# Weights split as rows and turned by transposing transfers, and another order of the head, in a gated feed-forward kernel with quantised activations

## The chip, the cores and the metric

One core of a Trainium2 chip runs the kernel; the other cores are idle. The metric is the device time of one execution in microseconds, the median of several runs. A profile of one execution shows what each engine did: TensorE (PE, with its weight loads as PEld), VectorE (DVE), ScalarE (ACT), GpSimd (POOL), and SyncE (SP), which here issues nearly all DMA transfers.

## What is computed

Cut to what matters, with B = 4 batches of S = 1024 tokens, D = 512, FF = 2048 and C = 128:

```
scale = cond @ norm_w.T + 1.0
ms = jnp.mean(x * x, axis=-1, keepdims=True)
h = x * (scale[:, None, :] * jax.lax.rsqrt(ms + EPS))
u = h @ up_w.T
val, gate = jnp.split(u, 2, axis=-1)
h = val * jax.nn.gelu(gate, approximate=False)
hq = h + stop_gradient(act_quant(h) - h)          # per token: round(x * 127 / max|x|), -128 to 127, back
wq = down_w + stop_gradient(weight_quant(down_w) - down_w)   # round(w / mean|w|), -1 to 1, back
y = hq @ wq.T
return y + x
```

All inputs and the output are float32. The first product must be nearly exact, because its result is rounded to integers.

## The kernel before

**Split products.** A float32 matrix is scaled by a power of two and split into two float16 parts, high and low ("w" counts the parts of the weights, "l" those of the tokens). A product is then the sum of high x high, high x low and low x high. The parts of the weights are wanted with D on the partitions, but `up_w` lies with FF as rows, so each block of weights has to be turned.

**Slots.** FF is cut into 16 blocks j of 128; a slot is one block of one batch of 1024 tokens, g = 16 b + j. Each slot has a gate block (t = 1) and a value block (t = 0).

**Batch 0** runs plain products (`plain`, `plain_half`): for each half of 512 tokens, 12 products for the gate into PSUM tag B or A, a Gelu on ScalarE, 12 products for the value into tag E (two banks), and one VectorE multiply (line 556) of value, gain and gate into `H`. While batch 0 runs, the weights of all 16 slots are prepared, two to four slots ahead (`first_batch`, slots 3 to 15):

- `w_load` brings 256 KB per t into `wn(j)`, one of three places; `w_range` finds each row's largest value on VectorE and its power of two (`w_factor`); `w_scale` scales the rows on GpSimd.
- `w_turn` turns the block on TensorE, 8 transposes of 128x128 float32 (line 296) into PSUM tag po. `w_high` (ScalarE) casts the high parts out of PSUM, `w_low` (VectorE) subtracts for the low parts; `w_evac` (ScalarE) copies the turned float32 to SBUF.
- `s_sums` makes four sums of the quarters of the block on GpSimd, `s_high` and `s_low` split them, and `s_spill` writes the slot's seven chunks (two float16 parts of 256 columns each) to `s_dram` in HBM in one transfer of 896 KB.
- Beside it the tokens of batch 1 are normalised, summed, split and turned by transposing transfers (`Tokens`: load, norm, scale, sums, high, low, turn), `down_w` is averaged and rounded (`d_load`, `d_sum`, `d_round`, `d_put`), and running maxima over pairs of slots are taken (`pair_max`).

**Batches 1 to 3** use seven products per slot in place of eight (a Strassen scheme, `slot` and `product`, 42 products of 512 columns in a slot of about 9.07 us), with the seven chunks read back from `s_dram`: `s_load_x` brings chunks 0 to 4 of slot g + 2, `s_load_y` chunks 5 and 6 of slot g + 1, both issued at the end of slot g. `SX` and `SY` say which chunk holds which operand. The second product (down) of the batch before runs inside slots 10 to 13.

**The head** prepares the first slot. Line 903 and what follows loads 8 tiles of tokens, `norm_w` and the weights of slots 0 to 2; warm products keep TensorE going; the sums of squares run on ScalarE, the reciprocal root (`rsqrt`) is a power on GpSimd, and the first 512 tokens are taken by quarters of the batch's half (two tiles of 128 at a time: `part_turn`, `part_high`, `part_low`, class `First`). Line 912 is a GpSimd power on a constant, ahead of the others.

**The order** of the work on every engine is the order of the program (`tc.manual_schedule()`): each engine and each DMA queue takes its instructions in that order and waits for what an instruction needs. SyncE's queue holds, in batch 0, the loads of weights, the spills, the turns of tokens and of `down_w`, and `cond_rows` in slot 3, three transfers of four-byte elements.

Of the kernel before, what the change touches and what calls it, by code (L numbers as in the profile page):

```python
# [14 lines left out]
ALU = mybir.AluOpType  # L15
# [22 lines left out]
SX = {0: 0, 1: 1, 4: 2, 5: 3, 6: 4}  # L38
# [12 lines left out]
def glu_quant_kernel(  # L51
# [81 lines left out]
    def s_tile(g):  # L133

        if g >= NJ:
            return SXY[:, (g + 1) % 2]
        return S_more if g % 3 == 2 else SXY[:, g % 3]
# [10 lines left out]
    def bank(tag, bufs, shape=None, name=None):  # L148
        return psum.tile(shape or [P, TOK], F32, name=name or tag, tag=tag, bufs=bufs)
# [102 lines left out]
    def wf(j):  # L252

        return H[:, 11 if j == 2 else 15 + j % 2].rearrange("p t (n f) -> p (t n) f", n=2)
# [3 lines left out]
    def w_load(j, ts=(1, 0)):  # L258
        for t in ts:
            SP.dma_start(out=wn(j)[:, t], in_=up_v[j][:, t])  # L260
# [21 lines left out]
    def w_scale(j, ts=(1, 0), eng=POOL):  # L282
        for t in ts:
            w, r = wn(j)[:, t], iv[j][:, t : t + 1]
            if eng is ACT:
                ACT.activation(w, w, AF.Copy, scale=r)
            else:
                eng.tensor_scalar(w, w, r, 1.0, ALU.mult, ALU.mult)  # L288
# [11 lines left out]
    def a_parts(j):  # L300

        s = s_tile(j)
        return s[:, 0:2], A21[:, j % 3], s[:, 5]
# [23 lines left out]
    def s_sums(j):  # L327
        a11, a12, a21, a22 = (wf(j)[:, n] for n in range(4))
        POOL.tensor_tensor(sf[:, 0], a21, a22, ALU.add)
        POOL.tensor_tensor(sf[:, 2], a11, a21, ALU.subtract)  # L330
        POOL.tensor_tensor(sf[:, 1], sf[:, 0], a11, ALU.subtract)
        POOL.tensor_tensor(sf[:, 3], a12, sf[:, 1], ALU.subtract)

    def s_parts(j):
        s = s_tile(j)
        return (s[:, 2:5], sf[:, 0:3]), (s[:, 6:7], sf[:, 3:4])
# [9 lines left out]
    def s_spill(j):  # L346
        SP.dma_start(out=s_dram[j], in_=s_tile(j).rearrange("p c w f -> p (c w f)"))

    CUT = 5 * 2 * HALF

    def s_load_x(g):
        s = s_tile(g)[:, 0:5].rearrange("p c w f -> p (c w f)")
        SP.dma_start(out=s, in_=s_dram[g % NJ, :, :CUT])

    def s_load_y(g):
        s = s_tile(g)[:, 5:7].rearrange("p c w f -> p (c w f)")
        SP.dma_start(out=s, in_=s_dram[g % NJ, :, CUT:])
# [181 lines left out]
    def gain(g, t):  # L539
        return sg[g // NJ][:, g % NJ, t : t + 1]  # L540

    def h_half(g, h):
        return h_slots(g)[:, 0, h]
# [14 lines left out]
    QT = TOK // 2  # L558

    class First:  # L560


        def __init__(self):
            self.ps = {1: bank("B", 1, name="pg_0_0"), 0: bank("A", 2, name="pv_0_0")}

        def part(self, t, q, w, l):
            gate, a21, a22 = a_parts(0)
            a = [gate[:, 0], gate[:, 1]] if t else [a21, a22]
            c = slice(q * QT, (q + 1) * QT)
            for k in range(NK):  # L570
                PE.matmul(
                    self.ps[t][:, c],
                    a[k // 2].rearrange("p w (k f) -> p w k f", k=2)[:, w, k % 2, :],
                    XP[:, l, k, c], start=w + l + k == 0, stop=l == 1 and k == NK - 1,
                )

        def gate(self):
            self.t1 = wpool.tile([P, TOK], F32, name="g_0_0", tag="t1")
            ACT.activation(self.t1, self.ps[1], AF.Gelu, scale=gain(0, 1))

        def value(self):
            DVE.scalar_tensor_tensor(
                h_half(0, 0), self.ps[0], gain(0, 0), self.t1, ALU.mult, ALU.mult
            )

# [249 lines left out]
    start_t = sm.tile([P, 1], F32, name="start_t", bufs=1)  # L835
    ACT.dma_start(out=cn, in_=cond[0:1])
    ACT.activation(start_t, one, AF.Gelu)
# [19 lines left out]

    def first_scale(n, eng):
        r = rs0[:, n : n + 1]
        if eng is ACT:  # L860
            ACT.activation(X0[:, n], X0[:, n], AF.Copy, scale=r)
        else:
            eng.tensor_scalar(X0[:, n], X0[:, n], r, 1.0, ALU.mult, ALU.mult)
# [5 lines left out]

    def part_turn(n, pts):  # L870
        for k in range(NK):
            c = k % 2 * QT + n % 2 * P
            PE.transpose(pts[k // 2][:, c : c + P], X0[:, n, k * P : (k + 1) * P], ident)

    def part_high(q, k, pts):
        c = slice(q * QT, (q + 1) * QT)
        v = pts[k // 2][:, k % 2 * QT : (k % 2 + 1) * QT]
        ACT.activation(XP[:, 0, k, c], v, AF.Copy, scale=scT[:, k, 0:1])

    def part_low(q, k, pts):  # L880
        c = slice(q * QT, (q + 1) * QT)
        v = pts[k // 2][:, k % 2 * QT : (k % 2 + 1) * QT]
        DVE.scalar_tensor_tensor(
            XP[:, 1, k, c], v, scT[:, k, 0:1], XP[:, 0, k, c], ALU.mult, ALU.subtract
        )
# [18 lines left out]
    SP.dma_start(out=nw, in_=norm_w.rearrange("(k p) c -> p k c", p=P))  # L904
    w_load(0, (1,))
    first_load(2, 2)
    w_load(0, (0,))
# [4 lines left out]
    POOL.tensor_tensor(rs0[:, 0:1], one, neghalf[:, 0:1], ALU.pow)  # L912
    keep_warm(3)
    pc = cond_first_row()
    keep_warm(7)
    first_sum(0)
    first_sum(1)
    cond_scale(0, pc)
    rsqrt(ssq0[:, 0:2], rs0[:, 0:2])
    mx = cond_largest(0, 1)  # L920
    pm = cond_over(mx, 0, 1, "A")
    am = w_largest(0, 1, 2)
    w_factor(0, am, 1, 2)
    first_scale(0, POOL)
    first_scale(1, ACT)
    dg = cond_range(pm, 0, 1)
    w_scale(0, (1,))
    ptx = [[po_bank("ptx_0_0"), po_bank("ptx_0_1")], [po_bank("ptx_1_0"), None]]
    part_turn(0, ptx[0])
    part_turn(1, ptx[0])  # L930
    pd = cond_spread(dg, 0, 1, "A")
    w_turn(0, [bank("E", 2, name=f"pw_0_{t}") for t in (1, 0)], (1,))
    ptx[1][1] = bank("A", 2, name="ptx_1_1")
    first_sum(2)
    first_sum(3)
    cond_undo(pd, 0, 1)
    rsqrt(ssq0[:, 2:4], rs0[:, 2:4])
    part_high(0, 0, ptx[0])
    w_high(0, (1,))
    for k in range(1, NK):  # L940
        part_high(0, k, ptx[0])
    first_scale(2, POOL)
    first_scale(3, POOL)
    w_low(0, (1,))
    w_range(0, 0, 1)
    w_scale(0, (0,))
    for k in range(NK):
        part_low(0, k, ptx[0])
    first = First()
    first.part(1, 0, 0, 0)  # L950
    first.part(1, 0, 1, 0)
    part_turn(2, ptx[1])
    part_turn(3, ptx[1])
    w_turn(0, ts=(0,))
    first.part(1, 0, 0, 1)
    w_high(0, (0,))
    for k in range(NK):
        part_high(1, k, ptx[1])
    w_gain(0)
    am = w_largest(1, 1, 2)  # L960
    w_low(0, (0,))
    for k in range(NK):
        part_low(1, k, ptx[1])
    w_factor(1, am, 1, 2)
    w_scale(1, (1,))
    w_range(1, 0, 1)
    w_gain(1)
    w_scale(1, (0,))
    cond_load_rest()
    for w, l in ((0, 0), (1, 0), (0, 1)):  # L970
        first.part(0, 0, w, l)
    for w, l in ((0, 0), (1, 0), (0, 1)):
        first.part(1, 1, w, l)
    first.gate()
    w_turn(1, ts=(1,))
    w_high(1, (1,))
    w_low(1, (1,))
    for w, l in ((0, 0), (1, 0), (0, 1)):
        first.part(0, 1, w, l)
    first.value()  # L980
    w_range(2)
    w_gain(2)
    w_scale(2)
    w_turn(1, ts=(0,))
    w_high(1, (0,))
    w_low(1, (0,))
# [12 lines left out]

    def first_batch(j, sc):  # L1000
# [5 lines left out]
        if j in TOKENS:  # L1006
            t = toks[j] = toks[j + 1] = Tokens(1, TOKENS[j])
            t.load()
        if j - 2 in TOKENS:
            toks[j - 2].turn()  # L1010
        t = toks.get(j)
        odd = t is not None and j not in TOKENS
        if j + 1 < NJ:
            s_sums(j + 1)
        if odd:
            t.sums()
        if j + 3 < NJ:
            w_range(j + 3)
            w_gain(j + 3)
            w_scale(j + 3)  # L1020
        if j == 5:
            part = d_total()
        plain_half(j, 0)
        if j == 3:
            pd = cond_spread(dg, 1, B, "po")
            cond_undo(pd, 1, B)
            cond_rows()
# [4 lines left out]
        if j + 1 < NJ:  # L1032
            s_high(j + 1)
            s_low(j + 1, POOL)
            s_spill(j + 1)
        if j + 2 < NJ:
            w_turn(j + 2)
            w_high(j + 2)
            w_evac(j + 2)
            w_low(j + 2)  # L1040
        plain_half(j, 1)
        if j == 5:
            d_mean(part)
        for i, h in pairs[2:]:
            for f in pair_max(0, i, h):
                f()
        if t and not odd:
            t.norm()
        if t and not odd:
            t.scale(sc)  # L1050
        for n in D_SUM.get(j, ()):
            d_sum(n)
        if j - 1 in D_ROUND:
            d_put(D_ROUND[j - 1])
        if odd:
            t.high()
            t.low(DVE)
        if j in D_ROUND:
            d_round(D_ROUND[j])
# [4 lines left out]


# [18 lines left out]
    def s_all(j):  # L1084
        s_high(j)
        s_low(j, POOL)
        s_spill(j)

# [50 lines left out]
    s_all(3)  # L1139
    for n in D_SUM[2]:  # L1140
        d_sum(n)
# [385 lines left out]
```

## Time and profile before

| | us |
|---|---|
| median of 3 runs (749.6 to 749.73) | 749.6 |
| the profiled execution, device time | 749.6 |
| its span, first to last instruction | 747.4 |
| head, to the first product of slot 1 | 0 to 26.9 |
| slots 1 and 2 and the second halves of 0 to 2 | 26.9 to 59.5 |
| batch 0, slots 3 to 15 | 59.5 to 204.6 |
| batches 1 to 3 and the last product down | 204.6 to 747.4 |

| engine | busy us | share | instructions |
|---|---|---|---|
| TensorE | 734.7 | 98% | 3781 |
| its weight loads | 374.6 | 50% | 3781 |
| VectorE | 601.7 | 81% | 872 |
| ScalarE | 382.2 | 51% | 646 |
| GpSimd | 218.3 | 29% | 227 |

The device time is 2.2 us more than the span; that lies around it. The clock that TensorE was granted averages 0.993 of full speed. Of the DMA traffic, 74.66 MB were read from HBM and 23.09 MB written. A group of the profile names a line, engine and operation, the tile written and the tiles read, and how often; "L556" is line 556 of the code. A releaser in brackets is what ended an engine's wait.

### The profile page before, as it was taken

What the parts mean: (1) busy time and instruction counts of PE and PEld (TensorE: products, weight loads), DVE (VectorE), ACT (ScalarE), POOL (GpSimd) and SP (SyncE); (2) the same over time, 40 slices, a digit from 0 to 9 for tenths busy, and PEclk for the clock granted to TensorE, in tenths of its full rate; (3) what the DMA queues carried; (4) which work ended last, traced back from release to release, by engine and by line L of the source; (5) the groups of instructions that cost most, each with busy time, mean ns of one, the idle gap of its engine ahead of it and who ended that gap; (6) DMA issues with size and microseconds to landing.
All of it is one profiled execution on the core that took longest, in us unless ns stands there. A gap on an engine that the chain in (4) does not pass through costs nothing.

```text
span 747.4 us, 10318 instructions
## 1 busy us (share of the span) xinstructions
PE 734.7 (98%) x3781; PEld 374.6 (50%) x3781; DVE 601.7 (81%) x872; ACT 382.2 (51%) x646; POOL 218.3 (29%) x227
## 2 busy tenths in 40 slices
PE   6899999999999999999999999999999999999998
PEld 3554554554444445566444445566444444445744
DVE  4776588978989899798679888787679888764897
ACT  3648546556234667444433667454433666333274
POOL 2479577989410030444010021444020000000100
PEclk7999999999999999999999999999999999999999
DMA  6259856566832425646933344566932333333253
GB/s 225 82 175 307 167 184 163 182 163 177 247 112 100 126 100 183 153 136 157 225 115 104 108 142 159 165 167 155 223 101 100 100 98 103 104 112 111 85 184 112
DMA packets 90141, 110.47 MB, mean 148 GB/s; under 512 B 57190, under 2 KB 58087, under 8 KB 90092
## 3 DMA queue, kind: packets, MB, share of 16 engines
q1 hardware_dynamic: 89802, 109.50, 49.3%
q8 instruction: 29, 0.48, 0.2%
q10 hardware_dynamic: 290, 0.33, 0.1%
q14 instruction: 20, 0.16, 0.1%
HBM read 74.66 MB, written 23.09 MB: 131 GB/s over the span
## 4 chain that ended last, share of the span: by engine, by line
PE 93%; DVE 3%; issue 2%; POOL 1%; DMA 1%; ACT 0%; SPq 0%; POOLq 0%; DVEq 0%
PE A L513 32%; PE E L513 16%; PE pv L528 11%; PE pg L528 10%; PE po L791 8%; PE B L513 8%; PE po_end L740 4%; PE pw L296 2%; PE po L740 1%; POOL H L288 1%; DMA R<-in_L_cond_norm_w_dram 1%; DVE gm L654 1%; PE po_B L791 0%; DVE R L656 0%; DVE R L649 0%
## 5 line engine op out<-in xcount | busy, mean ns | idle before, releaser
L513 PEld LDWEIGHTS <-SXY 128*128 128x128 f16 x2016 | 197.2, 98 | 232.4 <-issue 0.6
L513 PE MATMUL A<-R,SXY 128*128 128x512 f16 x1152 | 266.3, 379 | 0.0
L513 PE MATMUL E<-R,SXY 128*128 128x512 f16 x576 | 140.0, 379 | 0.1
L618 DVE SCALAR_TENSOR_TENSOR H<-A,sg,t 128x512 f32<-128x512 f32 x48 | 36.0, 750 | 72.0 <-PE A L513 71.8
L670 POOL PARTITION_ALL_REDUCE am<-R x8 | 14.3, 1793 | 223.4 <-DVE R L656 223.4
L712 DVE TENSOR_TENSOR H<-H,am 128x1024 f32<-128x1024 f32 x64 | 76.2, 1218 | 0.0
L631 ACT ACTIVATE t<-t,sg 128x512 f32<-128x512 f32 x48 | 34.6, 721 | 69.3 <-DVE t L628 69.2
L513 PE MATMUL B<-R,SXY 128*128 128x512 f16 x288 | 70.0, 379 | 0.0
L654 DVE TENSOR_REDUCE gm<-H 128x512 f32<-128x1024 f32 x56 | 69.0, 1232 | 1.0
L422 POOL TENSOR_TENSOR rs<-ssq,neghalf 128x2 f32<-128x2 f32 (+1 forms) x15 | 11.3, 754 | 189.8 <-DVE ssq L421 189.6
L528 PE MATMUL pv<-R 128*128 128x512 f16 x246 | 61.6, 379 | 0.0
L528 PEld LDWEIGHTS <-SXY 128*128 128x128 f16 x378 | 37.0, 98 | 42.1
L528 PE MATMUL pg<-R,SXY 128*128 128x512 f16 x252 | 57.8, 379 | 0.0
L791 PE MATMUL po<-wd,R 128*128 128x256 fp8e4 (+1 forms) x448 | 56.8, 275 | 0.0
L528 PEld LDWEIGHTS <-R 128*128 128x128 f16 x366 | 35.8, 98 | 41.8
L791 PEld LDWEIGHTS <-R 128*128 128x128 bf16 (+1 forms) x480 | 46.9, 98 | 12.9
L615 ACT ACTIVATE t<-B,sg 128x512 f32<-128x512 f32 x48 | 33.0, 687 | 36.1 <-PE B L513 36.1
L598 ACT COPY t<-A 128x512 f32<-128x512 f32 x48 | 27.9, 582 | 39.8 <-PE A L513 39.5
L606 ACT COPY B<-A 128x512 f32<-128x512 f32 x48 | 27.4, 572 | 39.0 <-PE A L513 38.4
L720 ACT ACTIVATE H<-H 128x1024 f32<-128x1024 f32 x38 | 39.9, 1050 | 14.2 <-DVE H L712 14.1
L656 DVE TENSOR_TENSOR R<-R,gm 128x512 f32<-128x512 f32 x56 | 42.9, 765 | 1.3
L610 ACT COPY v<-E 128x512 f32<-128x512 f32 x48 | 28.1, 585 | 30.9 <-PE E L513 27.6
(185 smaller groups left out, 1046.6 us busy)
## 6 DMA issues: line engine op xcount, KB each, us to landing
SXY<-s_dram SPq DMA_DIRECT2D x48, 640.0 KB, 3.9
SXY<-s_dram SPq DMA_DIRECT2D x48, 256.0 KB, 4.3
s_dram<-SXY SPq DMA_DIRECT2D x11, 896.0 KB, 4.8
H<-in_L_cond_up_w_dram SPq DMA_DIRECT2D x32, 256.0 KB, 5.1
xr<-in_x_dram SPq DMA_DIRECT2D x19, 256.0 KB, 2.9
out_dram<-xr SPq DMA_DIRECT2D x19, 256.0 KB, 4.5
s_dram<-R SPq DMA_DIRECT2D x5, 896.0 KB, 6.7
H<-in_x_dram SPq DMA_DIRECT2D x8, 512.0 KB
```

Source lines behind the costliest of these rows:

```text
L513: PE.matmul(o, s[:, w, k, :], tv[:, :, c, l, k, :], start=start and n == 0, stop=stop and n == len(TERMS) - 1, skip_group_check=True,)
L528: PE.matmul(ps, a[k // 2][:, w, k % 2, :], XP[:, l, k, h * TOK : (h + 1) * TOK], start=n == 0, stop=n == len(terms) - 1,)
L610: ACT.copy(cur["v"], cur["E"])
L615: ACT.activation(cur["t1"], pb, AF.Gelu, scale=gain(g, 1))
L618: DVE.scalar_tensor_tensor(h_half(g - 1, 0), prev["A"], gain(g - 1, 0), prev["t1"], ALU.mult, ALU.mult)
L631: ACT.activation(prev["t2"], prev["t2"], AF.Gelu, scale=gain(g - 1, 1))
L654: DVE.tensor_reduce(gm[0], v, AX.X, ALU.max, apply_absolute_value=True)
L656: return [largest, lambda: DVE.tensor_tensor(m, m, gm[0], ALU.max)]
L712: DVE.tensor_tensor(v, v, r.to_broadcast([P, 2, TOK]), ALU.mult)
L720: ACT.activation(v, v, AF.Copy, bias=MAGIC)
L740: PE.matmul(po.rearrange("p (y c o) -> p y c o", c=2, o=P), q[:, a, h, j], wd8[:, :, j // n, j % n, :, y0:y1].rearrange("p c o y -> p y c o"),
L791: PE.matmul(po, w[:, j], m, start=start and j == 0, stop=stop and j == n - 1, skip_group_check=True,)
```

## The change

Two things change.

1. For slots 5 to 15 (`ROWS = 5`) the weights are split into high and low parts as rows, before they are turned (`w_rows`: three casts on ScalarE, three subtractions on VectorE), and four of the chunks are turned by one transposing transfer out of SBUF. The sums are made from the rows, one slot earlier than before (`s_sums(j + 2)`), split, and spilled as rows; each of the 33 reads in batches 1 to 3 turns them by a transposing transfer from HBM. `w_scale` of these slots runs on ScalarE. The chunks are renumbered. In `first_batch` the token steps, `d_put` and `d_round` move ahead of the second half of the slot's products.
2. The head takes the first 512 tokens whole (`plain_first`), with the preparation of slots 0 and 1 called between its products; the reciprocal root is a ScalarE square root and a Newton step on VectorE (`rsqrt_start`); `norm_w` is loaded first; ScalarE starts with the table of the square root and changes to that of Gelu later.

```diff
-SX = {0: 0, 1: 1, 4: 2, 5: 3, 6: 4}
+SX = {4: 0, 5: 1, 6: 2, 0: 3, 1: 4}
...
     def w_load(j, ts=(1, 0)):
+        if j > 2:
+            SP.dma_start(out=wn(j), in_=up_v[j])
+            return
...
+    ROWS = 5
+
+    def w_scale(j, ts=(1, 0), eng=None):
+        eng = eng or (ACT if j >= ROWS else POOL)
...
     def a_parts(j):
 
         s = s_tile(j)
-        return s[:, 0:2], A21[:, j % 3], s[:, 5]
+        return s[:, 3:5], s[:, 6] if j >= ROWS else A21[:, j % 3], s[:, 5]
+
+    def w_row_parts(j):
+
+        v = H[:, 15 + j % 2].bitcast(F16).rearrange("p t d -> p (t d)")
+        v = v.rearrange("p (n w f) -> p n w f", n=4, w=2)
+        f = wn(j).rearrange("p t (n f) -> p t n f", n=2)
+        return (v[:, 0:2], f[:, 1]), (v[:, 2:3], f[:, 0, 1:2]), (v[:, 3:4], f[:, 0, 0:1])
+
+    def w_rows(j):
+        for o, f in w_row_parts(j):
+            ACT.copy(o[:, :, 0], f)
+        for o, f in w_row_parts(j):
+            DVE.tensor_tensor(o[:, :, 1], f, o[:, :, 0], ALU.subtract)
+        SP.dma_start_transpose(
+            s_tile(j)[:, 3:7].rearrange("p n w (k f) -> p (n w k) f", k=2),
+            H[:, 15 + j % 2].bitcast(F16).rearrange("p t d -> p (t d)"),
+        )
...
     def s_sums(j):
-        a11, a12, a21, a22 = (wf(j)[:, n] for n in range(4))
+        if j >= ROWS:
+            v = wn(j).rearrange("p t (n f) -> p t n f", n=2)
+            a11, a12, a21, a22 = v[:, 1, 0], v[:, 1, 1], v[:, 0, 0], v[:, 0, 1]
+        else:
+            a11, a12, a21, a22 = (wf(j)[:, n] for n in range(4))
...
     def s_spill(j):
-        SP.dma_start(out=s_dram[j], in_=s_tile(j).rearrange("p c w f -> p (c w f)"))
+        if j < ROWS:
+            SP.dma_start(out=s_dram[j], in_=s_tile(j).rearrange("p c w f -> p (c w f)"))
+            return
+        SP.dma_start(
+            out=s_dram[j, :, :Y_AT], in_=s_tile(j)[:, 0:6].rearrange("p c w f -> p (c w f)")
+        )
+        SP.dma_start(
+            out=s_dram[j, :, Y_AT:], in_=A21[:, j % 3].rearrange("p w f -> p (w f)")
+        )
+
+    Y_AT = 6 * 2 * HALF
+
+    def s_load(g, c0, c1, turn=False):
+        s, d = s_tile(g)[:, c0:c1], s_dram[g % NJ, :, c0 * 2 * HALF : c1 * 2 * HALF]
+        if turn:
+            SP.dma_start_transpose(s.rearrange("p c w (k f) -> p (c w k) f", k=2), d)
+        else:
+            SP.dma_start(out=s.rearrange("p c w f -> p (c w f)"), in_=d)
 
     def s_load_x(g):
-        s = s_tile(g)[:, 0:5].rearrange("p c w f -> p (c w f)")
-        SP.dma_start(out=s, in_=s_dram[g % NJ, :, :CUT])
+        if g % NJ < ROWS:
+            s_load(g, 0, 5)
+        else:
+            s_load(g, 3, 5)
+            s_load(g, 0, 3, True)
...
+    def plain_first(between):
+
+        ps = {1: bank("B", 1, name="pg_0_0"), 0: bank("A", 2, name="pv_0_0")}
+        gate, a21, a22 = a_parts(0)
+        order = [(1, w, 0, k) for w in range(2) for k in range(2)]
+        order += [(1, w, 0, k) for k in range(2, NK) for w in range(2)]
+        order += [(0, w, 0, k) for w in range(2) for k in range(NK)]
+        order += [(t, 0, 1, k) for t in (1, 0) for k in range(NK)]
+        for n, (t, w, l, k) in enumerate(order):
+            if n in between:
+                between[n]()
...
+    def rsqrt_start(t, y):
+
+        z = sm.tile([P, NA], F32, name="newton", bufs=1)
+        ACT.activation(z, t, AF.Sqrt, scale=1.0 / D, bias=eps)
+        DVE.tensor_scalar(t, t, 1.0 / D, EPS, ALU.mult, ALU.add)
+        DVE.reciprocal(y, z)
+        DVE.tensor_tensor(z, y, y, ALU.mult)
+        DVE.scalar_tensor_tensor(z, z, -0.5, t, ALU.mult, ALU.mult)
+        DVE.scalar_tensor_tensor(y, z, 1.5, y, ALU.add, ALU.mult)
...
+    def second_part():
+        w_turn(0, ts=(0,))
+        w_high(0, (0,))
+        w_low(0, (0,))
+        w_scale(1, (1,), ACT)
+        for k in range(1, NK):
+            first_low(0, k, ptx[k])
+        ACT.activation(start_t, neghalf[:, 0:1], AF.Gelu)
...
     def first_batch(j, sc):
...
-        if j in TOKENS:
-            t = toks[j] = toks[j + 1] = Tokens(1, TOKENS[j])
-            t.load()
-        if j - 2 in TOKENS:
-            toks[j - 2].turn()
...
-        if j + 1 < NJ:
+        n = j + 2
+        rows = ROWS <= n < NJ
+        if j + 1 < ROWS:
             s_sums(j + 1)
+        elif rows:
+            s_sums(n)
...
             w_range(j + 3)
             w_gain(j + 3)
-            w_scale(j + 3)
...
         plain_half(j, 0)
+        if j + 3 < NJ:
+            w_scale(j + 3)
...
-        if j + 1 < NJ:
-            s_high(j + 1)
-            s_low(j + 1, POOL)
-            s_spill(j + 1)
-        if j + 2 < NJ:
-            w_turn(j + 2)
-            w_high(j + 2)
-            w_evac(j + 2)
-            w_low(j + 2)
+        if j + 1 < ROWS:
+            s_all(j + 1)
+        elif rows:
+            s_all(n)
+        if n < ROWS:
+            w_turn(n)
+            w_high(n)
+            w_evac(n)
+            w_low(n)
+        if t and not odd:
+            t.norm()
+        if j - 1 in D_ROUND:
+            d_put(D_ROUND[j - 1])
+        if j in D_ROUND and j > 5:
+            d_round(D_ROUND[j])
+        if t and not odd:
+            t.scale(sc)
+        if odd:
+            t.high()
+            t.low(DVE)
+        if j + 1 in TOKENS:
+            toks[j + 1] = toks[j + 2] = Tokens(1, TOKENS[j + 1])
+            toks[j + 1].load()
+        if odd:
+            t.turn()
         plain_half(j, 1)
         if j == 5:
             d_mean(part)
+        if ROWS <= j + 3 < NJ:
+            w_rows(j + 3)
...
+    plain_first({6: second_part, 16: second_slot})
...
     s_all(3)
+    w_rows(5)
```

`s_load_y` splits in the same way (chunk 5 straight, chunk 6 turned), and `s_all` is `s_high`, `s_low` and `s_spill` of one slot. `second_slot`, called ahead of the seventeenth product, turns and splits the weights of slot 1 and finds the range and scale of slot 2's. In the head the order of issue on SyncE is now `norm_w`, tiles 0 to 3, the weights of slots 0 and 1, tiles 4 to 7, the weights of slot 2.

## The prediction

> **What bounds the kernel now.** I read the page first (engines, chain of waits), then the busy time in stretches cut at the slots of batch 0, then the timelines of VectorE, ScalarE and SyncE in those slots, then the DMA issues.
>
> ```profile
> PE 734.7 (98%) x3781; PEld 374.6 (50%) x3781; DVE 601.7 (81%) x872; ACT 382.2 (51%) x646; POOL 218.3 (29%) x227
> PE 93%; DVE 3%; issue 2%; POOL 1%; DMA 1%; ACT 0%; SPq 0%; POOLq 0%; DVEq 0%
> L296 PE MATMUL pw<-ident,H 128*128 128x128 f32 x128 | 18.4, 284 | 2.1 <-POOL H L288 2.1
> ```
>
> TensorE sets the end almost everywhere after 27 us. The third line is what the change attacks: the weight turns. Now the slots of batch 0 (stretch, length, then PE, PEld, DVE, ACT, POOL busy with counts, clock, DMA share, GB/s):
>
> ```profile
> 93.90:105.20 11.30, 11.30 (x58) 5.60 (x56) 10.45 (x17) 6.39 (x14) 7.74 (x9) 1.00 0.57 194
> 116.40:127.70 11.30, 11.30 (x58) 5.61 (x56) 11.16 (x19) 5.48 (x10) 6.85 (x9) 1.00 0.74 207
> 138.90:150.10 11.20, 11.20 (x57) 5.58 (x56) 11.00 (x18) 6.29 (x13) 9.81 (x11) 1.00 0.59 184
> 183.80:194.20 10.40, 10.40 (x50) 4.68 (x48) 9.59 (x12) 5.72 (x10) 10.11 (x10) 1.00 0.57 157
> ```
>
> A slot with a turn takes 11.24 us, one without 10.37 (183.83 to 194.19 in the chain), so a turn of eight costs 0.87. The third number to see is VectorE: 10.5 to 11.2 us busy in even slots (tokens), 7.4 to 10.1 in odd ones. TensorE leads, but VectorE is just behind, in order, and it waits:
>
> ```profile
> 88.39 1.22 DVE L265 TENSOR_REDUCE wam<-H 128x2 f32<-128x1024 f32 x1 [4.94 <-DMA H<-in_L_cond_up_w_dram]
> 130.17 0.17 DVE L421 TENSOR_SCALAR ssq<-ssq 128x2 f32<-128x2 f32 x1 [1.44 <-ACT xt L447]
> 154.36 0.17 DVE L421 TENSOR_SCALAR ssq<-ssq 128x2 f32<-128x2 f32 x1 [3.01 <-ACT xt L447]
> ```
>
> DMA issues (KB each, us to landing), and below them two turns as SyncE issues them (start, length), then the core's GB/s over 66 to 92 us in 40 slices:
>
> ```profile
> SXY<-s_dram SPq DMA_DIRECT2D x48, 640.0 KB, 3.9
> R<-nx SPq DMA_TRANSPOSE x8, 7.7
> wd<-tn SPq DMA_TRANSPOSE x4, 4.8
> rows_dram<-scT SPq DMA_DIRECT2D x3, 2.0 KB, 13.7
> ```
> ```profile
> 143.00 2.04 SPq L406 DMA_TRANSPOSE wd<-tn  x1
> 147.36 6.66 SPq L499 DMA_TRANSPOSE R<-nx  x1
> ```
> ```profile
> GB/s 77 452 375 198 221 151 356 429 403 246 366 416 169 203 165 22 0 0 44 22 11 11 44 22 22 44 187 342 367 403 448 391 433 419 362 366 370 126 28 28
> ```
>
> A transposing transfer holds SyncE for 2.04 us with 8 blocks of 128 columns and 4.1 to 6.7 with 28, so 0.15 to 0.25 us a block. And after the three transfers of four-byte elements that cond_rows issues at 69.0, the queue moves almost nothing from 76 to 82: the weights of slot 8, issued at 72.67 behind them, reach VectorE at 88.39.
>
> **The change part by part.**
>
> *Turns removed.* Slots 3 to 13 lose the turns of j = 5 to 15: 11 x 0.87 = 9.6 us of TensorE. With them go w_high, w_evac and w_low.
>
> *What replaces them.* ScalarE: three casts (0.58, 0.38, 0.38 by the rows of lines 309 to 312) and w_scale of 2 x 0.66, for w_high and w_evac (1.0 + 0.95): +0.4 us. GpSimd loses 1.36 a slot; it was 6.9 to 10.4 busy, so that buys nothing. VectorE: three subtractions of the same sizes, 1.26 us start to start when they read PSUM; both operands now lie in SBUF, not shown for these sizes; the nearest row is line 496, 0.42 to 0.9 us per operation: bounds 1.3 and 2.1, I take 1.57. So VectorE gains nothing while its slot shrinks from 11.24 to 10.37. SyncE: one turn of 16 blocks, 2.4 to 4 us, I take 3.4.
>
> *The order on VectorE and ScalarE in slots 6 to 13*, which decides. The range of the weights (2.3 us as at 135.69 to 138.47) stays ahead of the first product's multiply; w_scale now sits on ScalarE behind that range, and the token steps move ahead of the second half. Even slot on VectorE: range 2.3, multiply 0.67, wait, ssq 0.17, two roundings 2.25, token scale 2.3, multiply 0.67, rows 1.57. The wait: ScalarE, free only from the reciprocal (0.2 before the range's end), does w_scale 1.32, s_high 1.12, the squares 1.24, in sum 3.7 with handover 3.8, while VectorE has 0.87 to do: 2.9. Slot 12.8. Odd: range 2.3, multiply 0.67, roundings 2.25, wait, lows 3.0, multiply 0.67, rows 1.57; ScalarE does 1.32 + 1.12 + 0.95 + the first cast 0.5 = 3.9 against VectorE's 3.1, wait 1.0 with handovers. Slot 11.5. A pair of slots: 24.3, against 20.7 that TensorE would need and 22.5 now. Late next is the multiply of the second half: psum tag E has two banks, so the value product (j+1, 1) starts only after multiply (j, 1). Bounds of a pair: 23.0 (range 1.85, lows 2.1 as without GpSimd's traffic), 25.5 (rows 2.1).
>
> *The head.* norm_w goes first and lands about 3.6, tiles 0 and 1 at 5.1, 2 and 3 at 6.9 (256 KB per 1.1 us, as 4.08 to 5.18 now). Four squares of 0.63 end at 7.5; a square root and five small VectorE steps of 0.17 to 0.2 give all scales at about 8.9, where now GpSimd's pow gives two at 10.37 and two at 15.1. Scales 0.65 each, 16 turns at 0.11, the weight turn, the first cast of each: the first product at about 13.5 instead of 15.42. The 24 products (5.2 us) then wait for the lows: range of slot 1 (2.0), four lows of 0.67, one Gelu table load (1.28) on ScalarE beside them. Slot 1 starts at about 22 instead of 26.89: -4.9; bounds 0 and -8.
>
> The clock belongs to this:
>
> ```profile
> 6.40:9.80 3.40, 0.48 (x2) 0.08 (x1) 2.25 (x13) 0.00 (x0) 0.73 (x2) 1.00 1.04 393
> 16.60:20.00 3.40, 3.40 (x17) 3.14 (x17) 2.83 (x10) 0.00 (x0) 0.69 (x1) 0.50 0.05 19
> 20.00:26.90 6.90, 6.07 (x51) 4.47 (x50) 4.89 (x16) 3.38 (x8) 1.38 (x2) 1.00 0.31 84
> ```
>
> After a stretch with 0.48 us of TensorE work the clock is halved; after a full one, mostly turns, it is whole again. The new head keeps warm products and turns going in 6.4 to 13, so I take the whole clock; halved, the head is 2.8 later (17 turns and some 5 products at double time). The Trainium skill (TensorE: Matmul & The Clock Gate, Part 4) says that turns do not count as busy like products; the row of 16.6 to 20.0, with 1.1 us of products and 2.3 of turns before the release, disagrees, and by the page those 2.8 us would be added.
>
> *Weights of slot 8.* The 4.9 us do not arrive. SyncE now has the turn of slot 5 ahead of the cond_rows transfers, and that turn waits until the spill of slot 2 has left its tile: spill at 60.25 - 5 = 55.2, landing 6.7, 3.4 to issue, 2 for the loads: cond_rows at 67.4 instead of 69.0. They land 13.7 later, 81.1, and the stall ends with them. Then come spill 5 and the turn of slot 6, 2 to 2.5 each (896 KB and 512 KB at some 400 GB/s by the slices around the stall, less for turned blocks), and the weights themselves, 3 to 6 (5.1 is the median; 88.39 - 82.6 now): 88.1 to 92.1, I take 89.5 (now 88.39). Bounds 84 and 92.5. From there VectorE: range 2.3, multiply 0.7, wait for the second gate 2.3, multiply 0.7, rows 1.6, first rounding 2.25, sc 0.8: slot 6's range at 100.3.
>
> *Reads of batches 1 to 3.* 33 reads get 12 and 4 blocks turned: SyncE 0.3 + 2.6 + 0.4 + 1.0 of a 9.07 us slot where it has 0.75 now, and waits in nothing else. The x part is issued when product 6 of slot g ends and is wanted 9.07 + 1.30 later (product 4 of g + 2). Nearest rows: 4.8 for 8 blocks, 7.7 for 28, so 5.2 to 6 and 0.4 behind the straight part: hidden, 0 us. A turn out of HBM is in no row; bounds 0 and the second rival. The skill (DMA: Bandwidth & Descriptors, Why small descriptors are slow) speaks against 256-byte pieces read from HBM, 27% more bus time; by it my estimate of the landing becomes some 7 us, still hidden.
>
> Order of chunks, one w_load instead of two, the split spill and the moved token loads: nothing, under SyncE's idle time; their delay is in the 67.4.
>
> **Sum.** Slot 6's range at 100.3; slots 6 to 11 three pairs, 73, and 1.0 for the pair maximum in slot 7 that no wait covers (slot 6's is covered): slot 12's range at 174.3. Its second multiply ends 11.3 later, 185.6; then 0.1, the value product 2.59, and slots 14 and 15 at 10.37: batch 0 ends at 209.0 against 204.6 now. +4.4, and 0.8 for handovers that 24.3 leaves out (four pairs x 0.2): +5.2. The profiled run took 749.6 with a span of 747.4; it equals the median. 754.8.
>
> **Rivals.**
> 1. *TensorE stays the bound* (not slower): VectorE's waits are covered and slot 8's weights come by 84. Then 749.6 - 9.6 - 4.9 = 735.1; half of it gives 742. For: VectorE's busy sum of slots 6 to 13 is 79 us, TensorE's new need 83. Against: 95% of an in-order queue whose ScalarE partner waits for its range. It decides where a pair needs under 20.7 us.
> 2. *Turned reads come late* (much slower): a landing above 10.4 us stalls each of 33 slots; at 12 us 33 x 1.6 = 53: 803. For: no row shows a turn out of HBM. Against: 7.7 us for 2.3 times the blocks.
> 3. *The head decides*: if the weights of slot 8 do not, the halved clock gives 754.8 + 2.8 = 757.6; inside the forecast's range.
>
> **Numbers.** Forecast (VectorE's queue, slots of 11.5 to 12.8) 0.67, its own range 748.5 to 763: weights at 84 take 5.5 off, at 92.5 add 3; three pairs at 23.0 take 3.9, at 25.5 add 3.6; not all at once. Rival 1 and halves of it 0.22, rival 2 0.08, else 0.03. The range reaches down to halves of rival 1, 740, and to 766 above; under 740 lie 0.1, above 766 0.1. A measurement of this kernel tells 0.2%, 1.5 us, from no change: faster 0.23, same 0.08, slower 0.69.
>
> **What would show it.** Right: no weight turns for j above 4; batch 0's slots 6 to 13 at some 12.2 us with TensorE idle before value products, released by VectorE's multiply; VectorE waiting 2 to 3 us for the squares in even slots; slot 1 near 22 us; the range of slot 8's weights near 89; batches 1 to 3 as long as now. Wrong: slots of 10.4 (rival 1), or SXY turns that land after 10 us and stalls before product 4 (rival 2).

## The result, and the profile after

The changed kernel took 757.8 us, the median of 4 runs (757.0 to 760.2), against 749.7 for the kernel before in the same runs: a ratio of 1.0113, 95% interval 1.0089 to 1.0137. It is slower by 8.1 us. The profiled execution took 758.36, with a span of 756.6.

The page of the changed kernel, engines and chain of waits:

```profile
PE 728.1 (96%) x3676; PEld 362.4 (48%) x3676; DVE 607.1 (80%) x869; ACT 386.6 (51%) x647; POOL 204.4 (27%) x199
PE 77%; POOL 10%; issue 7%; ACT 2%; DMA 2%; DVE 2%; SPq 0%; POOLq 0%; DVEq 0%; ACTq 0%
```

TensorE lost 6.6 us of work, and its share of the chain fell from 93% to 77%: it no longer sets the end everywhere. The chain says POOL and issue where it goes through a loop of VectorE, ScalarE and GpSimd; which of them decides has to be read from the engines' own order. The weight turns are down from 128 to 40, as meant, by the groups of lines:

```profile
L305 PE MATMUL pw<-ident,H 128*128 128x128 f32 x40 | 6.0, 289 | 0.1
```

Cut by stages, from the first products of the slots (batch 1 of the kernel before starts at 204.4; the 204.6 of the table ahead of the prediction is 0.2 late):

| stage (profiled executions) | before | after | difference |
|---|---|---|---|
| start to slot 3 | 59.5 | 54.2 | -5.3 |
| slots 3 to 15 of batch 0 | 144.9 | 159.1 | +14.2 |
| batches 1 to 3 and the end | 543.0 | 543.3 | +0.3 |
| span | 747.4 | 756.6 | +9.2 |

All of the loss lies in slots 3 to 15. TensorE's timeline there shows where it stood still (start, length, last bracket: idle time before and what ended it):

```profile
76.96 2.75 PE L580 MATMUL pg<-R 128*128 128x512 f16 x12 [1.44 <-ACT g L604]
93.83 0.56 PE L440 MATMUL pmean<-wpart,one 128*128 128x1 f32 x2 [6.35 <-DVE wpart L435]
128.39 4.44 PE L580 MATMUL pv<-R 128*128 128x512 f16 x12 [3.51 <-DVE H L608]
152.87 2.75 PE L580 MATMUL pv<-R,SXY 128*128 128x512 f16 x12 [1.91 <-DVE H L608]
165.04 2.75 PE L580 MATMUL pv<-R 128*128 128x512 f16 x12 [1.66 <-DVE H L608]
177.85 2.75 PE L580 MATMUL pv<-R,SXY 128*128 128x512 f16 x12 [2.06 <-DVE H L608]
190.03 2.75 PE L580 MATMUL pv<-R,SXY 128*128 128x512 f16 x12 [1.66 <-DVE H L608]
```

The idle times add up to 18.6 us. Twelve products take 2.75 in this view; the twelve at 128.39 took 4.44, and those behind pmean 4.73: 3.7 us more, at half the clock. So -9.6 for the turns that went, +22.3 for these stalls, and +1.5 left over: +14.2. The timelines point to two causes, and the experiments test both. The first is one wait of VectorE in slot 5, for the weights of slot 8; SyncE's timeline shows why they came late, and VectorE's shows the wait:

```profile
68.01 1.62 SPq L231 DMA_DIRECT2D rows_dram<-scT  x3
70.83 0.35 SPq L379 DMA_DIRECT2D s_dram<-SXY  x1
71.28 13.22 SPq L326 DMA_TRANSPOSE SXY<-H  x1
84.60 0.53 SPq L381 DMA_DIRECT2D s_dram<-R  x1
85.23 0.38 SPq L384 DMA_DIRECT2D s_dram<-R  x1
85.66 1.20 SPq L261 DMA_DIRECT2D H<-in_L_cond_up_w_dram  x1
```
```profile
91.67 1.22 DVE L269 TENSOR_REDUCE wam<-H 128x2 f32<-128x1024 f32 x1 [6.55 <-DMA H<-in_L_cond_up_w_dram]
```

The transposing transfer of slot 6's weights sits on SyncE for 13.2 us behind the four-byte transfers of cond_rows, and the load of slot 8's weights goes out at 85.66. In the kernel before it was issued 13 us earlier:

```profile
72.67 1.00 SPq L260 DMA_DIRECT2D H<-in_L_cond_up_w_dram  x2
```

The second cause is the loop in slots 6 to 13. VectorE's timeline over one pair of slots, an even one from 129.53 and an odd one from 142.26 (lines of no weight are left out):

```profile
129.53 1.21 DVE L269 TENSOR_REDUCE wam<-H 128x2 f32<-128x1024 f32 x1
...
131.38 0.74 DVE L608 SCALAR_TENSOR_TENSOR H<-pv,sg,g 128x512 f32<-128x512 f32 x1
135.01 0.17 DVE L473 TENSOR_SCALAR ssq<-ssq 128x2 f32<-128x2 f32 x1 [2.88 <-ACT xt L499]
135.09 1.24 DVE L446 TENSOR_SCALAR R<-R,wsc 128x1024 f32<-128x1024 f32 x1
136.37 0.70 DVE L447 TENSOR_SCALAR R<-R 128x1024 f32<-128x1024 f32 x1
137.14 2.20 DVE L509 SCALAR_TENSOR_TENSOR xn<-xn,rs,sc 128x512 f32<-128x512 f32 x2
139.26 0.74 DVE L608 SCALAR_TENSOR_TENSOR H<-pv,sg,g 128x512 f32<-128x512 f32 x1
139.92 2.41 DVE L325 TENSOR_TENSOR H<-H 128x512 f16<-128x512 f32 x3
142.26 1.20 DVE L269 TENSOR_REDUCE wam<-H 128x2 f32<-128x1024 f32 x1
...
145.32 0.74 DVE L446 TENSOR_SCALAR R<-R,wsc 128x1024 f32<-128x1024 f32 x1
...
148.53 1.96 DVE L548 TENSOR_TENSOR nx<-xn,nx 128x512 f16<-128x512 f32 x2 [1.73 <-ACT nx L544]
```

The next even range starts at 154.53 and the one after it at 179.52: a pair takes 25.0 us, 20.0 of it busy. VectorE waits 2.9 us for the squares in each even slot and 1.7 for the token casts in each odd one. ScalarE has them behind w_scale, and w_scale starts at 131.38 and 144.66, when VectorE's range ends. The first of the two in ScalarE's timeline, with its wait for the reciprocal (line 278) that closes the range:

```profile
131.38 1.33 ACT L295 ACTIVATE H<-H,iv 128x512 f32<-128x512 f32 x2 [5.74 <-DVE iv L278]
```

The turned reads of batches 1 to 3 and the other transfers, by the view of issues (median us from issue to landing):

```profile
SXY<-s_dram SPq DMA_TRANSPOSE x66, 3.1
R<-H SPq DMA_TRANSPOSE x8, 6.5
SXY<-H SPq DMA_TRANSPOSE x7, 4.5
rows_dram<-scT SPq DMA_DIRECT2D x3, 2.0 KB, 14.6
```

The reads land in 3.1 us, where 10.4 were to be had.

### The profile page after: what moved, and what is told of

It is laid out like the page before. It is cut to its first block, busy times and chain, and to the rows that moved or that the text cites. A ratio compares the mean times of both kernels' runs of the same rounds, so it can differ in the third digit from the quotient of the medians.

```text
span 756.6 us, 10152 instructions
## 1 busy us (share of the span) xinstructions
PE 728.1 (96%) x3676; PEld 362.4 (48%) x3676; DVE 607.1 (80%) x869; ACT 386.6 (51%) x647; POOL 204.4 (27%) x199
## 4 chain that ended last, share of the span: by engine, by line
PE 77%; POOL 10%; issue 7%; ACT 2%; DMA 2%; DVE 2%; SPq 0%; POOLq 0%; DVEq 0%; ACTq 0%
PE A L565 33%; PE E L565 16%; PE B L565 8%; PE po L836 8%; PE po_end L785 4%; PE pv L580 2%; PE pg L580 2%; POOL SXY L375 2%; POOL H L362 1%; POOL H L361 1%; POOL R L375 1%; POOL H L360 1%; DMA s_dram<-SXY 1%; POOL H L359 1%; DMA H<-in_x_dram 1%
## 5 line engine op out<-in xcount | busy, mean ns | idle before, releaser
L565 PEld LDWEIGHTS <-SXY 128*128 128x128 f16 x2016 | 197.1, 98 | 232.5 <-DMA SXY<-s_dram 0.7
L580 PEld LDWEIGHTS <-SXY 128*128 128x128 f16 x462 | 45.7, 99 | 61.8 <-issue 9.8
L580 PE MATMUL pg<-R,SXY 128*128 128x512 f16 x252 | 59.8, 389 | 0.0
L580 PE MATMUL pv<-R,SXY 128*128 128x512 f16 x210 | 49.9, 379 | 5.7 <-DVE H L608 5.6
L836 PEld LDWEIGHTS <-R 128*128 128x128 bf16 (+1 forms) x480 | 47.0, 98 | 12.8
L580 PEld LDWEIGHTS <-R 128*128 128x128 f16 x282 | 28.0, 99 | 40.9 <-issue 9.4
L765 ACT ACTIVATE H<-H 128x1024 f32<-128x1024 f32 x38 | 39.9, 1050 | 14.2 <-DVE H L757 14.1
L580 PE MATMUL pv<-R 128*128 128x512 f16 x162 | 40.6, 392 | 5.2 <-DVE H L608 5.2
```

The source lines that it names most:

```text
L565: PE.matmul(o, s[:, w, k, :], tv[:, :, c, l, k, :], start=start and n == 0, stop=stop and n == len(TERMS) - 1, skip_group_check=True,)
L580: PE.matmul(ps, a[k // 2][:, w, k % 2, :], XP[:, l, k, h * TOK : (h + 1) * TOK], start=n == 0, stop=n == len(terms) - 1,)
L765: ACT.activation(v, v, AF.Copy, bias=MAGIC)
L836: PE.matmul(po, w[:, j], m, start=start and j == 0, stop=stop and j == n - 1, skip_group_check=True,)
```

## The experiments

Each ran beside the kernel before on one chip; its median was 749.3 to 749.7, so two experiments can be compared to some 0.4 us. Stages and timelines are those of one profiled execution each.

**1. The rows taken out, the head kept.** The weights of all slots are turned by TensorE again; the new order inside the slots stays too.

```diff
-    ROWS = 5
+    ROWS = NJ
...
     s_all(3)
-    w_rows(5)
```

> All 16 slots' weights turned by TensorE again (ROWS = NJ), the new head and the new order of the token steps kept. Queue theory (the rows and the wait for slot 8's weights cost the time, the head is a gain): slot 3 stays 5.3 us earlier than in the kernel before and TensorE is busy from there on, so 749.7 - 5.3 = 744.4, within 743.5 to 746. Rival, the head or the new order of the steps is what costs: 749 or more.

Measured: 741.67 us (741.4 to 742.0), ratio 0.9901 (0.9886 to 0.9916). The chain of its page:

```profile
PE 98%; DMA 1%; ACT 0%; DVE 0%; issue 0%; SPq 0%; DVEq 0%
```

After the first products TensorE waits for nothing, and slots 3 to 15 take 144.9 us, as before the change. So the head is a gain of 8.0 here, and the rows with their transfers are a loss of 16.1. The gain is larger than the expected 743.5 to 746: first product at 13.86, slot 3 at 51.9 instead of 54.2, because the first tokens landed earlier in this execution (first square at 6.34 against 6.99 in the changed kernel's) and the clock was whole all through the head.

**2. The four-byte transfers on another queue.**

```diff
-            SP.dma_start(out=rows_dram[b]...
+            ACT.dma_start(out=rows_dram[b]...
```

> The changed kernel, with the three four-byte transfers of cond_rows issued on ScalarE's queue instead of SyncE's. Queue theory: the transposing transfer of slot 6, which held SyncE from 71.28 to 84.50, passes in some 3 us, the weights of slot 8 no longer come last, VectorE's wait of 6.5 us for them and TensorE's idle 6.35 before pmean go: 757.8 - 6.5 = 751.3, within 749 to 753. Rival, SyncE is held by the transposing transfers themselves: the weights come as late and the time stays at 757 to 758. Rival, the four-byte packets slow all queues: the same.

Measured: 763.03 (760.8 to 763.7), slower than the changed kernel. This was a miss. The core's traffic in 4 us stretches (last three columns: clock, DMA share, GB/s), and VectorE's waits:

```profile
64.00:68.00 4.00, 4.00 (x20) 1.78 (x19) 3.19 (x6) 3.13 (x6) 1.20 (x1) 1.00 1.47 169
68.00:72.00 4.00, 4.00 (x20) 1.84 (x19) 2.67 (x4) 0.76 (x4) 3.94 (x5) 1.00 0.96 22
72.00:76.00 4.00, 2.03 (x10) 0.71 (x8) 0.00 (x0) 3.95 (x7) 3.85 (x5) 1.00 0.98 42
```
```profile
78.28 1.22 DVE L269 TENSOR_REDUCE wam<-H 128x2 f32<-128x1024 f32 x1 [7.61 <-DMA H<-in_L_cond_up_w_dram]
...
93.45 1.22 DVE L269 TENSOR_REDUCE wam<-H 128x2 f32<-128x1024 f32 x1 [5.13 <-DMA H<-in_L_cond_up_w_dram]
```

The DMA engines are busy (share 0.96 to 0.98) and move 22 to 42 GB/s: the small packets hold up the transfers of both queues, whichever of the two they are in. Issued earlier, at 63.7, they now also catch the weights of slot 7, so VectorE waits twice. The Trainium skill (DMA: Bandwidth & Descriptors, Issuing engines are not separate DMA queues) says that transfers started by different engines run on the same 16 DMA engines; this run agrees.

**3. w_scale behind the token steps.**

```diff
         plain_half(j, 0)
-        if j + 3 < NJ:
+        if j + 3 < ROWS:
             w_scale(j + 3)
...
         if odd:
             t.turn()
+        if ROWS <= j + 3 < NJ:
+            w_scale(j + 3)
         plain_half(j, 1)
```

> The changed kernel, with w_scale of slots 5 to 15 issued on ScalarE behind the token steps of the slot, so that the casts of the sums, the squares and the casts of the tokens no longer queue behind a step that waits for VectorE's range. Queue theory: VectorE's waits of 2.9 (even) and 1.7 us (odd) go, a pair of slots falls from 25.0 to the 20.7 of TensorE, and of TensorE's idle 10.8 us ahead of value products after 94 us some 10 go: 748, within 746 to 750.5. Rival, VectorE has too much work whatever the order (its subtractions and roundings run beside GpSimd's sums): at most 2 us, 755.8 to 758. Rival, SyncE's transposing transfers set the pace: no change.

Measured: 750.05 (747.3 to 751.7), 7.7 less than the changed kernel, of some 10 expected. In VectorE's timeline the step that waited 2.88 now follows at once, but the rows are longer, and so is an operation on two columns:

```profile
128.12 0.74 DVE L608 SCALAR_TENSOR_TENSOR H<-pv,sg,g 128x512 f32<-128x512 f32 x1
128.78 0.16 DVE L473 TENSOR_SCALAR ssq<-ssq 128x2 f32<-128x2 f32 x1
...
132.86 2.98 DVE L325 TENSOR_TENSOR H<-H 128x512 f16<-128x512 f32 x3
...
138.06 1.48 DVE L284 TENSOR_SCALAR sg<-sw,dx 128x2 f32<-128x2 f32 x1
```

A pair is 22.5 us (126.27 to 148.78), not 20.7. The waits were real, and they were the larger part. TensorE's stall ahead of pmean, for slot 8's weights, grew from 6.35 to 8.40, so some of the gain was lost there. Behind the waits stood the rival: VectorE's work itself, made longer by GpSimd (a multiply of 128x2 elements takes 0.21 us elsewhere).

**4. Both edits**, 2 and 3 together.

> Both of the two edits before in one kernel. Queue theory: the two stalls are apart in time and add up, 757.8 - 6.5 - 10 = 741, within 738 to 744, so faster than both kernels. Rival, VectorE has too much work: 749 to 752, because only the wait for the weights goes.

Measured: 755.09 (753.9 to 756.1), 5.0 above the run with the late w_scale alone and outside both expected ranges, a miss. With the four-byte packets still in the way the first edit costs here too: VectorE waits 12.9 us for the weights of slot 7.

**5. The reads made straight.**

```diff
-            s_load(g, 0, 3, True)
+            s_load(g, 0, 3)
...
-            s_load(g, 6, 7, True)
+            s_load(g, 6, 7)
```

> The changed kernel, with the 33 reads of batches 1 to 3 made straight: their four chunks are not turned, which leaves the turning of those operands out of the computation. Queue theory: the turned reads are hidden, so within 1.5 us of 757.8. Rival, they cost TensorE a wait in each slot or slow other transfers: 754 or less.

Measured: 756.57 (756.3 to 757.2). In the profiled execution slots 3 to 15 take 159.6 us and what follows 543.2, against 159.1 and 543.3: turning at each read costs nothing that can be seen.

**6. The same data in 512-byte rows.**

```diff
-        for b in range(1, B):
-            SP.dma_start(out=rows_dram[b].rearrange("(k p) -> p k", p=P), in_=scT[:, :, b])
+        pr = po_bank("prows", [NK * B, P])
+        PE.transpose(pr, scT.rearrange("p k b -> p (k b)"), ident)
+        rt = sm.tile([NK * B, P], F32, name="rows_t", bufs=1)
+        ACT.copy(rt, pr)
+        SP.dma_start(out=rows_dram.rearrange("b (k p) -> k b p", p=P), in_=rt)
```

> The changed kernel, with cond_rows turned by TensorE first and written as 16 rows of 512 bytes instead of 1536 elements of four bytes. On ScalarE's queue the same four-byte transfers stalled everything as long as on SyncE's (the core moved 18 to 54 MB per ms from 68 to 76), so the stall is now put down to the packets, not to the queue. Theory: without them the weights of slot 8 come some 10 us earlier, VectorE's wait of 6.5 us goes, with it TensorE's idle 6.35 and the halved clock behind it: 757.8 - 6.5 = 751.3, within 748 to 752.5. Rival, SyncE held by its transposing transfers: 756 to 758.

Measured: 750.15 (749.4 to 752.1), 7.6 less than the changed kernel. SyncE's timeline:

```profile
67.87 0.76 SPq L234 DMA_DIRECT2D rows_dram<-rows_t  x1
...
71.10 6.82 SPq L329 DMA_TRANSPOSE SXY<-H  x1
...
79.07 1.16 SPq L264 DMA_DIRECT2D H<-in_L_cond_up_w_dram  x1
```

The weights of slot 8 are issued 6.6 us earlier, VectorE takes their range at 84.61 without a wait (91.67 in the changed kernel), and slot 6's range starts at 95.74 instead of 102.81. The transposing transfer still holds SyncE for 6.8 us at this place and for 1.9 in later slots; why isn't shown.

**7. 512-byte rows and late w_scale.**

> The 512-byte rows and w_scale behind the token steps together. Theory: the run with w_scale moved took 750.05 and has TensorE idle for 8.4 us before pmean and at half the clock for 12 products behind it (2.0 us): 750.05 - 10.4 = 739.6, within 737 to 743, so at or below the 741.7 of the kernel with the weights turned by TensorE. Rival, VectorE's work is the next bound right there: 745 or more.

Measured: 741.53 (740.8 to 744.1), ratio 0.9903 (0.9884 to 0.9923). The two mends add up (7.6 + 7.7 against 16.3 together), and the kernel draws level with the one whose weights TensorE turns. One pair of slots of this kernel, and two of experiment 1 (stretch, length, busy PE, PEld, DVE, ACT, POOL, clock, DMA share, GB/s):

```profile
142.50:165.04 22.54, 22.18 (x103) 9.99 (x102) 22.19 (x31) 14.60 (x27) 18.05 (x18) 1.00 1.02 260
```
```profile
96.50:119.00 22.50, 22.50 (x114) 11.19 (x113) 21.59 (x36) 13.02 (x27) 19.42 (x21) 1.00 0.60 168
119.00:141.50 22.50, 22.50 (x114) 11.25 (x113) 21.02 (x30) 14.01 (x28) 20.30 (x22) 1.00 0.74 199
```

A pair is 22.5 us in both. In the lower two TensorE fills it, as it does from 21 us on. In the upper one VectorE is busy all the time (22.2 of 22.5); TensorE, which stood still for 3.3 us at 121, works off what it is behind (103 products, where a pair has 96) and waits for VectorE again at 165.

**8. GpSimd's sums left out.**

```diff
     def s_sums(j):
         if j >= ROWS:
+            return
```

> The changed kernel without GpSimd's four sums for slots 5 to 15, which leaves these sums out of the computation (their splits and spills stay). Theory: VectorE's subtractions of 128x256 take 0.94 us beside a sum and 0.41 alone, its roundings 1.24 and 0.74; a pair of slots has about 1.1 us of this in the rows, 0.5 in the roundings, 0.9 in the lows, 2.5 in sum, and it lies on VectorE's path: 3.3 pairs take 8 us off, 750, within 747 to 753. Rival, only the order and the waits count: 756 to 758.

Measured: 745.62 (744.0 to 748.5), 12 less, and below the expected 747 to 753. A pair falls from 25.0 to 22.2, by 2.8 where 2.5 were expected, with both waits as they were (2.89 and 1.73). The profiled execution's head was 2.8 us earlier besides (slot 3 at 51.4), which has nothing to do with the edit; slots 3 to 15 take 147.4 instead of 159.1. TensorE's stalls of 1.44 and 3.51 and the halved clock behind the second are gone, and the four later ones shrink to 0.2 to 0.8; the one ahead of pmean stays (7.29). So the expectation named the right mechanism and counted too little for it.

**9 and 10. Less work on VectorE, with rows and with turns.**

```diff
-    def d_round(n):
-        DVE.tensor_scalar(dn, dn, wsc, 1.0, ALU.mult, ALU.min)
-        DVE.tensor_scalar(dn, dn, -1.0, MAGIC, ALU.max, ALU.add)
+    def d_whole(n):
+        ACT.activation(dn, dn, AF.Copy, scale=wsc, bias=MAGIC)
+    def d_clip(n):
+        DVE.tensor_scalar(dn, dn, MAGIC + 1.0, MAGIC - 1.0, ALU.min, ALU.max)
```

`d_whole` runs right behind the first half of the slot, `d_clip` where `d_round` was.

> The kernel with 512-byte rows and the late w_scale, and one of the two VectorE operations of d_round moved to ScalarE (scaled and rounded there by adding MAGIC, then clipped by one VectorE operation). In the run with the late w_scale VectorE worked without a wait from 85 to 178 us, 22.5 us a pair of slots, while TensorE needs 20.7. Theory: VectorE's work is now the bound; the moved operation takes 0.75 us a slot off it, 1.5 a pair, so a pair falls to 21.0 and some 3.5 pairs save 5: 736.5, within 735 to 739. Rival, ScalarE's 1.05 us more a slot turn into a new wait of VectorE, or the pair was held by the weights' transfers: 740.5 or more.

> The same kernel with all slots' weights turned by TensorE (ROWS = NJ). Theory: TensorE bounds batch 0 there (it waited for nothing after 22 us in the first run of this kind), so less work on VectorE brings nothing: 741.7, within 740.7 to 742.7. Rival, VectorE's work counts there too: 739 or less.

Measured: with rows 739.37 (738.3 to 741.2), ratio 0.9869 (0.9852 to 0.9885); with turns 745.01 (742.6 to 745.9). The first is the fastest kernel of the study, 1.3% below the kernel before, though it misses the expected 735 to 739 by a little. Its median is 2.2 us below that of experiment 7, not 5. In the profiled executions slots 3 to 15 took 138.8 us, against 143.6 in experiment 7, a fall of 4.8; but these two are the fastest of the four runs here (738.26, in spite of a late head with slot 3 at 54.1) and the slowest there (744.06), and what made up the rest in the other runs isn't shown. A pair of slots took 21.3 to 21.7, not 21.0, with one wait of VectorE for weights (1.62) among them.

With turns, the time lies above the expected 740.7 to 742.7, a miss. Slots 3 to 15 took 146.0, 1.1 more than without the edits; a wait of 0.88 for the new copy in cond_rows is in it, and less work on VectorE brought nothing. What else lies between its profiled execution and that of experiment 1 is the head: slot 1 at 24.3 instead of 21.0, with the clock at half from 13 to 20.

## Why the prediction was right, and where it was off

754.8 was forecast and 757.8 measured; the cause named as likeliest, VectorE's queue with its waits for ScalarE and for slot 8's weights, is the one that the runs show. Several terms were off in both directions, and that they nearly cancel is luck.

**Turns and head.** The turns went, and nothing was gained by it because TensorE stopped being the bound; where VectorE was relieved (experiment 9) slots 3 to 15 fell 6.1 below the kernel before, towards the 9.6. The head was to bring 4.9 by slot 1 and brought 3.5 (slot 1 at 23.4, not 22). By slot 3 it was 5.3, mostly because the weight turns of slots 1 and 2 no longer wait: in the kernel before TensorE stood still for 0.34 and 1.03 ahead of two of them. The forecast hadn't counted that. The head's steps were off: the first product came at 16.20, not 13.5, since the first tokens landed at 7.0 rather than 5.1; and the clock that I took as whole was 0.50 from 13 to 16. In other executions of the same head it was whole, and slot 3 started between 51.4 and 52.7, or it was halved, up to twice as long, and slot 3 started between 53.9 and 55.2.

**Weights of slot 8.** cond_rows were to be issued at 67.4 and were at 68.0; the range came at 91.7 instead of 89.5, inside the bounds of 84 and 92.5. Behind the stall I had one spill and the turn of slot 6 at 2 to 2.5 us each, and then the load at 3 to 6. The turn sat on SyncE until 84.5, the load went out at 85.66, and VectorE had the weights 6.0 later, at the upper end. The wait for the second gate (2.17) was foreseen, but its price is partly the halved clock behind pmean (4.73 for 12 products). Slot 6's range: 102.8, not 100.3.

**The order on VectorE and ScalarE.** The even slot was 12.73 (12.8 forecast), with the wait at 2.88 (2.9). The wait was foreseen; the sum is partly luck, as its rows took 2.3 instead of 1.57, while the range took 1.85 instead of 2.3 and roundings and scaling were 0.4 shorter. The range was also misread: 135.69 to 138.47, the lines named for 2.3, are 2.8. The odd slot was 12.27 (11.5): its wait was 1.7 instead of 1.0, the lows 3.6 instead of 3.0, and the rows at its end 1.8 instead of 1.57; its two roundings, with GpSimd idle, took 1.5 instead of 2.25. The term that was mis-sized is *rows 1.57*: there is no one duration. Three subtractions take 1.34 us when GpSimd is idle and 2.41 when it adds; I took one value for all slots, and the longer one is even past my upper bound of 2.1. A pair was 25.0 instead of 24.3, inside 23.0 to 25.5. Batch 0 ended at 213.3 instead of 209.8: slot 6's range was 2.5 late, the six slots behind it took 76.7 instead of 74.0, and what followed made up 1.7.

**Reads.** Hidden, as forecast; they landed in 3.1 us, faster than the 5.2 to 6 that rows of other turns gave. Experiment 5 shows no cost, and batches 1 to 3 took 543.3 against 543.0.

**Rivals.** Rival 1 asked for waits of VectorE that are covered and weights by 84: experiment 7 has both nearly so and reaches 741.5, the "half of it" of 742, but not 735, as VectorE's own work then fills 22.5 us. Rival 2 is out by the landings of 3.1 us and by experiment 5. Rival 3 counted the halved clock in the head as 2.8; it does occur, and slot 3 starts 1.2 to 3.8 us later in the executions that have it, though their first products are later too (15.6 to 16.2 against 13.4 to 14.7), so how much is the clock's isn't shown.

## What to carry to other kernels

Work taken off the bounding engine is worth only what the next in-order queue lets through: before moving it, lay out that queue with its partners, and put a step that waits (here w_scale, for a range) behind the steps that don't. Transfers of four-byte elements stalled the transfers of both queues here, so write them as rows, and do it before adding transfers that come due behind them. A VectorE operation on two SBUF operands had two prices here, alone and beside GpSimd; take both from the trace, by place.

## What the runs showed of the hardware

**VectorE beside GpSimd.** VectorE's subtraction of 128x256 float32 took 0.41 us with GpSimd idle and 0.94 in every case where a GpSimd sum ran all through it; the scaling of 128x1024 (line 446) 0.74 and 1.21 to 1.24, once 2.1. The first of the three subtractions of 139.92 below, 128x512, began before the sum of 140.01 and took 0.68 as alone; the two behind it took 0.94. At 69.5, beside GpSimd's subtractions of line 375, VectorE's took 0.41, and there GpSimd's two took 3.5 us, against 2.3 at 146.80. The Trainium skill (SBUF — State Buffer, Who interferes with whom) has the two engines exclude each other when VectorE reads two SBUF tensors and GpSimd reads SBUF as well; the subtractions agree. Two stretches of the changed kernel's timelines, VectorE's and GpSimd's, show it:

```profile
128.26 1.34 DVE L325 TENSOR_TENSOR H<-H 128x512 f16<-128x512 f32 x3
```
```profile
138.75 1.17 POOL L361 TENSOR_TENSOR H<-H 128x256 f32<-128x256 f32 x1
140.01 1.18 POOL L362 TENSOR_TENSOR H<-H 128x256 f32<-128x256 f32 x1
141.15 0.91 POOL L520 TENSOR_TENSOR xt<-xn 128x256 f32<-128x256 f32 x1
```

GpSimd has nothing between 128.26 and 133.51; the rows of 139.92 (2.41 us, shown above) run beside these three.

**The clock after a stall.** TensorE ran at half the clock for some 4 us behind the stall of 6.35 us, and in the head, where it stood still for 2.9 us ahead of the turns. Both stretches of the changed kernel, with the clock as the third column from the end:

```profile
13.00:16.00 3.00, 2.53 (x13) 2.13 (x11) 0.78 (x4) 1.12 (x2) 0.83 (x2) 0.50 0.30 110
94.20:96.60 2.40, 2.40 (x7) 0.91 (x8) 0.23 (x2) 2.40 (x6) 0.93 (x1) 0.50 0.81 202
```

The length of a single idle time doesn't decide. Behind idle times of 1.3 to 2.07 us twelve products took 2.75; behind 2.08 (experiment 2) 4.42 and behind 2.36 (experiment 3) 4.23; but behind 2.77 (experiment 4, ahead of pmean) 2.75. What the traces show is a grid: in each execution the granted clock changes only at times that lie multiples of 3.41 us apart (in the changed kernel at 12.96, 16.37, 91.47, 98.29, 129.01 and 132.43), and what counts is the idle time inside one such stretch. The 2.08 of experiment 2 fell into one stretch, and the next was at half the clock (the first two lines). The 2.77 of experiment 4 were split by a border, 1.28 and 1.49 (the other two):

```profile
177.16:180.57 3.41, 1.33 (x7) 0.53 (x6) 3.41 (x5) 1.66 (x4) 3.33 (x3) 1.00 0.91 224
180.57:183.98 3.41, 3.41 (x10) 1.21 (x9) 3.24 (x8) 0.81 (x2) 0.22 (x1) 0.50 1.61 256
```
```profile
92.81:96.22 3.41, 2.13 (x10) 0.78 (x8) 0.86 (x2) 2.11 (x5) 1.53 (x1) 1.00 0.97 314
96.22:99.64 3.42, 1.93 (x10) 1.02 (x11) 2.19 (x8) 2.23 (x4) 1.50 (x4) 1.00 1.02 271
```

In the heads and batch 0 of the twelve profiled executions, every stretch with 2.08 us or more of idle time was followed by half the clock, and none at the whole clock with 1.91 or less was; of three in between, with 2.03 to 2.06, two were. A stretch of turns without any product (experiment 6, 12.34 to 15.75) was followed by the whole clock, so turns alone can bring it back; in experiments 7 and 10 a stretch of mostly turns, from 13.2 and 13.0, with 0.7 idle, didn't, and why isn't shown. The Trainium skill (TensorE: Matmul & The Clock Gate, Why this matters for your kernels) warns of gaps above some 3 us; here 2.08 were enough, and the measurement decides.

What stays open: why the first tokens land between 5.5 and 7.0 us after the start wasn't tried. The head's clock doesn't follow from that alone: with tokens at 5.8 it fell to half in experiment 10, with tokens at 6.3 it stayed whole in experiment 1.
